# Layer 0's scan as a second row of stages, half an image ahead

## The chip, the cores and the metric

The kernel runs on one core of a Trainium2 chip. A core has five engines that work beside each other, each through its own instructions in order: PE (matmul), DVE, ACT and POOL (elementwise work), and SP, which issues the DMAs here. The metric is the time of one execution on the device in microseconds, as the median of several runs; smaller is better.

## The reference

The input is eight images of 64 x 64 tokens with 192 channels. Two layers follow each other.

Layer 0 projects to 384 channels, runs a 3 x 3 depthwise convolution with SiLU, and then a chunked state-space scan in two directions (six heads of 64 channels, 32 states, one decay per head and token). The result is gated with SiLU, projected, and an MLP of 768 hidden channels follows, with residuals.

Layer 1 splits the channels. Half of them pass a branch of three convolutions with batch norms. The other half is normalized, projected to 192 channels, convolved depthwise, and scanned selectively in four directions (row and column order, each forwards and backwards):

```python
def step(h, t):
    u_t, d_t, b_t, c_t = t
    h = jnp.exp(d_t[..., None] * A) * h + (d_t * u_t)[..., None] * b_t[:, :, None, :]
    return (h, jnp.einsum('bkdn,bkn->bkd', h, c_t))
```

Here d_t is a softplus of a projection, A is a constant for each of 192 channels and 16 states, and 4096 tokens are scanned. The four results are summed, normalized, gated, projected, and laid beside the branch's channels with a residual.

## The kernel before, in words

The backbone is `selective_scan` (L1167). It cuts the scan of one image into 8 steps of 1024 tokens (four forwards, four backwards), each step into 3 tiles of 128 channel-directions, each tile into 16 units of 8 channels x 16 states: 384 units an image, 3072 in all. For one unit q:

- `fetch` (L1314) loads delta, repeated over the states, into dA, four units ahead and into five buffers; `decay` makes exp(delta A) of it on ACT.
- `spread` (L1324) forms delta u, repeated over the states, with two matmuls from three bf16 terms (`dus`) into dB in PSUM. There are two dB buffers.
- `weigh` (L1342) multiplies dB by the B rows on DVE; `scan` (L1347) runs the recurrence on DVE into h and multiplies h by the C rows on POOL.
- `gather` (L1365) sums over the states with matmuls, for four units at once and two units behind; `store` writes y to DRAM.

`prepare` (L1249) makes delta and delta u of the next tile during the current one: softplus on ACT and POOL for all 1024 tokens, delta to DRAM, delta u in three bf16 terms to DRAM, and twelve copies back into `dus`. Its pieces are placed by half-units 0 to 31 of the tile; delta u's terms go out at 20, its copies at 23, and the first matmul that needs them stands at 30. `project` makes B, C and delta's rank terms of the next step.

All other work is written as Python generators that yield their PE cost in microseconds, or None for "no more in this half-unit". The order of instructions on each engine is fixed by the order in which the pieces are called (`pin`); no scheduler changes it. `Beside` (L1130) holds one list of such stages. In each half of a unit `half` gives it a credit, the image's total cost over its half-units, and runs the first stage until the credit is spent or it yields None. Beside image b's scan run, one after another: for image b+1 layer 0's convolution (`conv0`), layer 0's scan (`ssd`, 32 chunks of 128 tokens, four chunks in flight through five steps), its MLP (`mlp0`); for image b-1 the branch (`conv_branch`), with `scan_sums` on the side, and `scan_outputs`; and for image b+1 `scan_inputs` and `transposed`, which write the scan's input u to DRAM. Before the next image's first load, `finish` issues at once what is left. The first image's stages run alone ahead of the scan, and the last image's sums and outputs alone behind it.

PSUM has eight banks. dB takes four. The other four are handed out in turn by `Shared.one` (L87); eight of them are in turn while the first image's stages run alone.

Of the kernel before, what the change touches and what calls it, by code (L numbers as in the profile page):

```python
# [16 lines left out]
HH = WW = 64  # L17
# [12 lines left out]
S = 64  # L30
Q = 2 * S
NC = L // Q
GC = 8
# [8 lines left out]
NXP = 4 * NS + 2 * RK  # L42

# [31 lines left out]
class Shared:  # L75
# [5 lines left out]
    def __init__(self, tc):  # L81
        self.tc, self.nc, self.pin = tc, tc.nc, tc.keep_in_program_order
        self.k = {}
        self.singles = []
        self.side = None

    def one(self, name):  # L87

        self.singles.append(self.singles.pop(0))
        return self.singles[-1].tile([128, 512], F32, tag="n", name=name)  # L90

    def aside(self):

        for piece in self.side or ():
            if piece is None:
                return True
        self.side = None
        return False
# [10 lines left out]
def setup(cx, cp, dp, p0, p1):  # L109
# [122 lines left out]
    for n, c0, c1 in (("xa", 0, 128), ("xb", 128, DI), ("za", DI, DI + 128), ("zb", DI + 128, 2 * DI)):  # L232
# [3 lines left out]
        nc.vector.tensor_copy(k["bias_" + n][: c1 - c0], ps[: c1 - c0, 0:1])  # L236
    nc.vector.tensor_scalar_mul(k["in_proj"], k["in_proj"], ln_g)
# [37 lines left out]
    k["xrows"] = dp.tile([L, INNER0], F32, tag="xrows", name="xrows")  # L275
    k["prows"] = dp.tile([L, 2, NP0], F32, tag="prows", name="prows")
    k["yrows"] = [dp.tile([L, INNER0], F32, tag=f"yrows{d}", name=f"yrows{d}") for d in range(2)]
# [49 lines left out]
def conv0(cx, x):  # L327

    nc, pin, k = cx.nc, cx.pin, cx.k
    NP, R2 = NB // 2, 2 * RB  # L330
    with cx.pool("cw0") as wp, cx.pool("v0", 2) as vp:
# [13 lines left out]
        first = vp.tile([CH, 2, R2 * WW], F32, tag="xt", name="first")[:, :, :WW]  # L345
# [3 lines left out]
        def load(p):  # L349

            n = min(R2, HH - 1 - p * R2)
            xts[p] = vp.tile([CH, 2, R2 * WW], F32, tag="xt", name="xt")
            at = (p * R2 + 1) * WW
            pin(nc.sync.dma_start(
                out=xts[p][:, :, : n * WW], in_=x[:, at : at + n * WW].rearrange("(a p) l -> p a l", p=CH)
            ))

        def rows_in(j, src, n, at):
# [8 lines left out]
            ))  # L367

        def project(p, j):
# [5 lines left out]
            for b in range(2):  # L375
                n = min(RB, HH - 1 - p * R2 - b * RB)
                if n < RB:
                    pin(nc.gpsimd.memset(pad[:, R2 + 1, :], 0.0))
                rows_in(j, xts[p][:, :, b * RB * WW : (b * RB + n) * WW], n, 2 + b * RB)
                yield 2.4  # L380

        def convolve(p, j):
            pss = [cx.one("ps_cv") for i in range(2)]
            yield from depthwise(cx, pss, [diag[0:64, j], diag[64:128, j]], pads[j])
            for i, ps in enumerate(pss):
                xc = xcs[p, 2 * j + i] = vp.tile([128, 512], F32, tag="xc", name="xc", bufs=7)
                pin(nc.scalar.activation(xc, ps, AF.Silu, bias=k["cb"][:, 2 * j + i : 2 * j + i + 1]))
            cx.exp_again()

        def turn(p, q):  # L390

            here = slice(q * 128, (q + 1) * 128)
            xo = vp.tile([128, 2, INNER0], F32, tag="xo", name="xo")
            po = vp.tile([128, 2, 2 * NP0], F32, tag="po", name="po")
            for g in range(2):
                ps = cx.one("ps_x")
                for i in range(3):
                    pin(nc.tensor.transpose(ps[:, i * 128 : (i + 1) * 128], xcs[p, 3 * g + i][:, here], k["ident"]))
                pin(nc.scalar.copy(  # L399
                    xo[:, :, g * 192 : (g + 1) * 192].rearrange("t b (i c) -> t b i c", i=3),  # L400
                    ps[:, : 3 * 128].rearrange("t (i b c) -> t b i c", b=2, c=64),
                ))
                yield 0.6
            pss = [cx.one("ps_p") for b in range(2)]
            for i in range(2 * NJ):
# [6 lines left out]
                if i % 3 == 2:  # L412
                    yield 1.4
            for b in range(2):
                pin(nc.scalar.copy(po[:, b, :], pss[b][:, : 2 * NP0]))
            yield None
            for rows, t in ((k["xrows"], xo), (k["prows"].rearrange("l k m -> l (k m)"), po)):
                at = p * R2 * WW
                dst = rows[at : at + R2 * WW].rearrange("(b q t) c -> q t b c", b=2, t=128)[q]
                pin(nc.sync.dma_start(out=dst, in_=t))  # L420
# [18 lines left out]
def ssd(cx):  # L439
# [7 lines left out]
    nc, pin, k = cx.nc, cx.pin, cx.k  # L447
    K2 = 2 * NH
    chunks = [slice(i * S, (i + 1) * S) for i in range(2)]
    states_of = [slice(d * N0, (d + 1) * N0) for d in range(2)]  # L450

# [3 lines left out]
    with cx.pool("g0", 2) as gp, cx.pool("s0", 2) as sp:  # L455
        H = sp.tile([2 * N0, NH, HP], F32, tag="H", name="H", bufs=4)
        pin(nc.sync.dma_start(out=H, in_=k["p0_h0"].rearrange("n (h p) -> n h p", p=HP)))
        state = {0: H}
        groups, st = {}, {}

        def group(g):

            both = gp.tile([128, GC, 2, 2, N0], F32, tag="both", name="both")
            raw = gp.tile([128, GC, 2, NH], F32, tag="raw", name="raw")
            for d in range(2):
                for i, (at, dims) in enumerate(token_rows(k["prows"], d, g * GC, GC)):
                    def rows(col, n):
                        return bass.AP(k["prows"].tensor, k["prows"].offset + at + d * NP0 + col, dims + [[1, n]])

                    for bc in range(2):  # L470
                        pin(nc.sync.dma_start(out=both[chunks[i], :, bc, d, :], in_=rows(bc * N0, N0)))
# [1135 lines left out]
```

## Time and profile before

| What | us |
| --- | --- |
| Median of 3 runs (17,945.96 to 18,016.35) | 17,987.26 |
| Profiled execution, its own time | 17,986.38 |
| Span of its instructions | 17,984.4 |
| First scan of the selective scan starts | 981 |
| Last one ends | 17,754 |
| Busy PE, DVE, POOL, ACT | 14,375.7, 12,309.3, 12,008.5, 10,711.9 |
| One scan on DVE (L1352), 3072 of them | 2.343 |
| One product h C on POOL (L1356), 3072 of them | 2.354 |
| One product dB B on DVE (L1345), 3072 of them | 1.218 |

A line of the profile's groups gives the source line, the engine, the operation, what it writes and reads, shapes, count, busy time and mean duration, and then the time its engine stood idle ahead of it with what ended that. A line of a window answer gives the stretch, its length, each engine's busy time with the number of instructions in brackets, the share of PE's clock that was granted, the mean busy share of the 16 DMA engines, and GB/s. A line of the waits reads: who waited, for whom, microseconds in total, how often, the longest. "SPq" is SP's queue. Busy shares are averages over stages with different limits, so the stages have to be looked at one by one.

### The profile page before, as it was taken

To read this page: it belongs to the slowest core of one execution; us is meant where nothing else is said; L and a number is where in the kernel's file an instruction comes from. 1 tells how busy PE (TensorE), PEld (TensorE's weight loads), DVE (VectorE), ACT (ScalarE), POOL (GpSimd) and SP (SyncE) were. 2 spreads that over 40 slices of the span, in tenths; PEclk is the share of its full clock that TensorE was granted. 3 is DMA by queue.
4 is the path that set the end of the run, shared out by engine and by line. 5 is a ranking of instruction groups with operands and counts; after the bars stand their busy time and mean duration, and the time that the engine had idled before them with its cause. 6 is when DMAs were issued, how large, how long until landed. Compare 5 with 4: busy or idle time off the path is not lost. (4 is left out here: it accounts for less than half of the span.)

```text
span 17984.4 us, 224777 instructions
## 1 busy us (share of the span) xinstructions
PE 14375.7 (80%) x76904; PEld 5676.6 (32%) x76904; DVE 12309.3 (68%) x9392; ACT 10711.9 (60%) x18482; POOL 12008.5 (67%) x6437
## 2 busy tenths in 40 slices
PE   8977788788877888778878788787888778868776
PEld 4623332343223431334313342233422334211111
DVE  2167787776667766677657775677766777667785
ACT  2464676466664756647566485664756557555654
POOL 3168776776668755687657875678755786657774
PEclk9987788789787887878878798787987779877676
DMA  3277777777677776777767777777776777677785
GB/s 85 75 201 177 189 190 202 168 193 199 170 195 174 192 194 164 196 176 201 186 170 188 176 199 185 184 188 178 197 183 178 184 183 198 180 194 190 184 196 143
DMA packets 1600969, 3238.93 MB, mean 180 GB/s; under 512 B 391580, under 2 KB 869396, under 8 KB 1596244
## 3 DMA queue, kind: packets, MB, share of 16 engines
q1 hardware_dynamic: 1599828, 3224.55, 71.2%
q8 instruction: 614, 10.06, 0.3%
q14 instruction: 527, 4.32, 0.1%
HBM read 2545.63 MB, written 678.18 MB: 179 GB/s over the span
## 5 line engine op out<-in xcount | busy, mean ns | idle before, releaser
L1356 POOL TENSOR_TENSOR h<-h,bc 128x1023 f32<-128x1023 f32 x3072 | 7223.5, 2354 | 3926.6 <-DVE h L1352 3412.2
L1352 DVE TENSOR_TENSOR_SCAN h<-dA,carry,dB 128x1024 f32<-128x1024 f32 x3072 | 7198.8, 2343 | 624.0 <-ACT dA L1322 188.7
L1345 DVE TENSOR_TENSOR dB<-dB,bc 128x1024 f32<-128x1024 f32 x3072 | 3741.5, 1218 | 2996.7 <-PE dB L1330 2948.1
L1322 ACT ACTIVATE dA<-dA,neg_a 128x1024 f32<-128x1024 f32 x3072 | 3486.8, 1135 | 797.5 <-DMA dA<-dld 795.3
L1374 PE MATMUL acc<-h,gather 128*32 128x512 f32 x12288 | 2479.9, 758 | 525.7 <-POOL h L1356 203.2
L1378 ACT COPY y<-acc 128x512 f32<-128x512 f32 x1536 | 886.5, 577 | 1908.7 <-PE acc L1374 1891.4
L1330 PE MATMUL dB<-dus,spread 24*128 24x512 bf16 x6144 | 1418.8, 430 | 365.3 <-DVE h L1352 283.8
L795 PE MATMUL ps_c<-p,conv_w 96*96 96x512 f32 x2304 | 1250.9, 670 | 120.5 <-ACT p L816 105.8
L1330 PEld LDWEIGHTS <-spread 24*128 24x128 bf16 x6144 | 317.6, 93 | 2607.9 <-issue 1700.3
L620 PE MATMUL ps_y<-dtx,M 64*64 64x64 f32 x12288 | 824.3, 267 | 393.5 <-DVE Hn L611 387.1
L1363 ACT ACTIVATE h<-h,bc 128x1 f32<-128x1 f32 x3072 | 905.1, 295 | 163.3 <-ACT carry L1362 3.8
L620 PEld LDWEIGHTS ps_y<-dtx,M 64*64 64x64 f32 x12288 | 691.6, 177 | 572.8 <-issue 349.5
L1374 PEld LDWEIGHTS acc<-h,gather 128*32 128x32 f32 x12288 | 321.2, 119 | 1690.8 <-issue 836.4
L319 PE MATMUL ps_cv<-pad,diag 64*64 64x512 f32 x6912 | 849.9, 611 | 5.6 <-ACT xo L399 2.8
L1276 POOL TENSOR_TENSOR w<-w,e 128x1024 f32<-128x1024 f32 x192 | 452.6, 2357 | 510.7 <-ACT carry L1362 423.7
L757 PE MATMUL ps_m<-h,w 128*96 128x256 f32 x3072 | 750.1, 392 | 30.2 <-DVE gT L715 20.4
L739 PE MATMUL ps_h<-o,w 96*128 96x256 f32 x3072 | 749.3, 397 | 4.3 <-ACT zs L697 1.7
L1362 ACT COPY carry<-h 128x1 f32<-128x1 f32 x3072 | 575.4, 187 | 250.9 <-DVE h L1352 248.1
L739 PEld LDWEIGHTS ps_h<-o,w 96*128 96x128 f32 x3072 | 585.6, 196 | 174.6 <-issue 62.3
L795 PEld LDWEIGHTS ps_c<-p,conv_w 96*96 96x96 f32 x2304 | 367.5, 177 | 814.8 <-issue 703.3
L555 PE MATMUL ps_d<-R,after 128*128 128x384 f32 x1024 | 554.8, 631 | 84.6 <-DVE M L575 36.8
L106 ACT ACT_TABLE_LOAD x481 | 617.1, 1283 | 8.2
(244 smaller groups left out, 22124.1 us busy)
## 6 DMA issues: line engine op xcount, KB each, us to landing
dA<-dld SPq DMA_DIRECT2D x3072, 512.0 KB
dud<-terms SPq DMA_DIRECT2D x192, 768.0 KB
dus<-dud SPq DMA_DIRECT2D x2304, 64.0 KB
bc<-bcd SPq DMA_DIRECT2D x256, 512.0 KB
X<-xrows SPq DMA_DIRECT2D x1024, 96.0 KB
yrows<-yo SPq DMA_DIRECT2D x1024, 96.0 KB
y<-yrows SPq DMA_DIRECT2D x256, 384.0 KB
u<-u SPq DMA_DIRECT2D x192, 512.0 KB
```

The costliest lines, as they stand in the source:

```text
L319: pin(nc.tensor.matmul(ps[64 * b : 64 * (b + 1)].rearrange("p (h w) -> p h w", w=WW), lhsT=diag[:, t, :], rhs=pad[64 * i : 64 * (i + 1), b ...
L620: pin(nc.tensor.matmul(psy[d][here, h * HP : (h + 1) * HP], lhsT=M[here, d, h, :], rhs=dtx[here, d, h, :], start=True, stop=d == 1,))
L739: pin(nc.tensor.matmul(ps[:, n * T : (n + 1) * T], lhsT=w1[:, a, (f + n) * 128 : (f + n + 1) * 128], rhs=o[:, a, :], start=a == 0, stop=a ...
L795: pin(nc.tensor.matmul(ps.rearrange("p (h w) -> p h w", w=WW), lhsT=w[:, t, :], rhs=pad[:, dy : dy + RB, dx : dx + WW], start=t == 0, stop ...
L1322: pin(nc.scalar.activation(dAs[q], dAs[q], AF.Exp, scale=k["neg_a"][:, steps[m][1], t, i : i + 1]))
L1330: pin(nc.tensor.matmul(dBs[q][:, half, :], lhsT=k["spread"][at : at + 3 * UD, :], rhs=du_of[n][at : at + 3 * UD, i // 2, :], start=True, s ...
L1345: pin(nc.vector.tensor_mul(dBs[q], dBs[q], of(q)[0]))
L1352: pin(nc.vector.tensor_tensor_scan(order(h, g), order(dA, g), order(dB, g), carry, ALU.mult, ALU.add))
L1356: pin(nc.gpsimd.tensor_mul(h[:, rest], h[:, rest], C_[:, rest]))
L1363: pin(nc.scalar.activation(end, end, AF.Identity, scale=C_[:, last : last + 1]))
L1374: pin(nc.tensor.matmul(ps[32 * v : 32 * (v + 1)], lhsT=k["gather"], rhs=hs[q - 3 + v][:, here], start=True, stop=True))
L1378: pin(nc.scalar.copy(y[:, here], ps))
```

## The change

`ssd` is rewritten and gets a row of its own in `Beside`. It works one chunk at a time in `front` and `back`, with a None after nearly every matmul group; in the prologue a chunk's back and the next one's front take turns (`together`). Its groups hold four chunks (`GC`) where they held eight, its pools stay open for the whole kernel, and layer 0's rows in DRAM exist twice. Each half-unit, `half` first gives the ssd row a share and then the other row the rest of the credit. A stage can name what it comes after. The other row runs `conv0` two images ahead, then the sums and outputs of the image before, then `mlp0`, `scan_inputs` and `transposed` of the next image; the branches are spread over images 0, 5, 6 and 7 as one, one, two and four. Image 1's `conv0` is woven into image 0's `ssd` in the prologue. `one` and `drop` hand PSUM banks out in the order in which their last readers were issued. `prepare` works in two halves of 512 tokens; delta u's second half goes out at half-unit 24, the copies for the tile's first eight units at 25, and those for the other eight in the next tile (`lay_du`). y is copied and stored in halves. Several tiles in the other stages have fewer buffers.

```diff
     def one(self, name):
-        self.singles.append(self.singles.pop(0))
-        return self.singles[-1].tile([128, 512], F32, tag="n", name=name)
...
+        home = self.free.pop(0)
+        t = home.tile([128, 512], F32, tag="n", name=name)
+        self.home[id(t)] = t, home
+        return t
+
+    def drop(self, *tiles):
+        for t in tiles:
+            self.free.append(self.home.pop(id(t))[1])
...
+    def front(c):
...
+        yield 0.4
+        yield None
+        bc = sp.tile([2 * N0, 2, Q], F32, tag="bc", name="bc", bufs=bufs)
+        pin(nc.scalar.copy(bc.rearrange("p i t -> p (i t)"), ps[: 2 * N0, : 2 * Q]))
+        cx.drop(ps)
...
+            yield 1.1
+            yield None
+            pin(nc.scalar.activation(flat(M[:, d]), some, AF.Exp))
+            cx.drop(ps)
...
+    def back(c):
+        next(coming, None)
...
+            yield 0.5
+            yield None
+            pin(nc.vector.tensor_add(H, ps[: 2 * N0, :INNER0].rearrange("p (h c) -> p h c", c=HP), H))
+            cx.drop(ps)
...
+    if not two:
+        for c in range(NC):
+            yield from front(c)
+            yield from back(c)
+        return
+    yield from front(0)
+    for c in range(NC):
+        yield from together(back(c), *([front(c + 1)] if c + 1 < NC else []))
...
     def half(self):
-        self.cx.aside()
         self.credit = min(self.credit, self.rate) + self.rate
-        while self.credit > 0.0 and self.stages:
-            for cost in self.stages[0]:
-                if cost is None:
-                    return
-                self.credit -= cost
-                if self.credit <= 0.0:
-                    return
-            self.stages.pop(0)
+        if self.ssds:
+            key, _, _, mine = self.ssds[0]
+            theirs = 0.0
+            for other in self.others:
+                if other[2] == key:
+                    break
+                theirs += max(other[3], 0.0)
+            mine = max(mine, 5.0)
+            self.share = min(self.share + (self.rate - 0.65) * mine / (mine + theirs), 2.0)
+            if self.share > 0.0:
+                spent = self.run(self.ssds, self.share)
+                self.share -= spent
+                self.credit -= spent
+        if self.credit > 0.0:
+            self.credit -= self.run(self.others, self.credit)
...
-            dl, e, w, b = (wp.tile([128, LC], F32, tag=v, name=v) for v in ("dl", "e", "w", "b"))
...
+            for at, here in zip((0, 12), halves):
+                dl, e, w, b = (wp.tile([128, 512], F32, tag=v, name=v) for v in ("dl", "e", "w", "b"))
...
+                yield at + 12
+                pin(nc.sync.dma_start(out=dud.rearrange("s p l -> p s l")[:, :, here], in_=terms))
+            yield 25
+            lay_du(n, 0)
+
+        def lay_du(n, part):
+            dus = np_.tile([128, UN // 4, 512], BF16, tag=f"dus{part}", name=f"dus{part}", bufs=1)
             for half in range(2):
                 for odd in range(2):
                     at = 32 * (2 * odd + half)
                     for v in range(3):
+                        rows = dud_of[n][v][64 * part : 64 * (part + 1), halves[half]]
                         pin(nc.sync.dma_start(
...
+                if at == 1:
+                    lay_du(n, 1)
...
                 for half in range(2):
+                    beside.half()
                     next(gathering, None)
-                    beside.half()
...
+    branches = list(range(B))
+    for b in range(B):
+        if b + 2 < B:
+            add("conv0", b + 2)
+        if b > 0:
+            add("sums", b - 1, ("scan", b - 1))
+            add("outputs", b - 1)
+        for _ in range({0: 1, B - 3: 1, B - 2: 2, B - 1: 4}.get(b, 0)):
+            add("branch", branches.pop(0))
+        if b + 1 < B:
+            beside.add(("ssd", b + 1), lambda b=b: ssd(cx, b + 1, gp, sp), ("conv0", b + 1))
+            add("mlp0", b + 1, ("ssd", b + 1))
+            add("inputs", b + 1)
+            add("transposed", b + 1)
+
+    def new_image(b, units):
+        rates, halves = [], 0
+        for i in range(b, B):
+            halves += 2 * (units if i == b else U_IMAGE)
+            key = ("transposed", i + 1) if i + 1 < B else ("branch", B - 1)
+            rates.append(beside.left(key, OWN * halves) / halves)
+        beside.rate = max(rates)
```

## The prediction

> **What bounds the kernel now.** The page first: no engine is full, and the chain that ended last names none.
>
> ```profile
> PE 14375.7 (80%) x76904; PEld 5676.6 (32%) x76904; DVE 12309.3 (68%) x9392; ACT 10711.9 (60%) x18482; POOL 12008.5 (67%) x6437
> PE 14%; DMA 10%; ACT 7%; POOL 6%; DVE 6%; issue 3%; SPq 1%; DVEq 0%; POOLq 0%; ACTq 0%
> ```
>
> So I cut the third image (5118 to 7315 us) by stage with the stage windows. In order: layer 0's convolution (48 scan units), the start of its scan (16), its scan (80), hand-over (17), its MLP (81), branch and sums (65), outputs and layer 1's inputs (80). The eighth row is a late stretch with hardly anything beside the selective scan (49 units). The units are the same windows' counts of L1352.
>
> ```profile
> core 0: us, PE busy (x) PEld busy (x) DVE busy (x) ACT busy (x) POOL busy (x), PEclk, DMA share, GB/s
> 5118.00:5333.00 215.00, 193.77 (x1282) 73.01 (x1282) 168.61 (x96) 157.29 (x284) 153.61 (x75) 0.89 0.79 203
> 5333.00:5454.00 121.00, 75.21 (x594) 36.51 (x594) 68.36 (x59) 57.56 (x126) 79.42 (x55) 0.70 0.68 156
> 5454.00:5943.00 489.00, 361.77 (x3452) 167.59 (x3452) 382.94 (x385) 222.32 (x434) 421.18 (x262) 0.78 0.71 176
> 5943.00:6045.00 102.00, 76.03 (x384) 45.83 (x381) 65.28 (x52) 68.55 (x103) 62.18 (x30) 0.82 0.77 197
> 6045.00:6423.00 378.00, 337.97 (x1472) 185.37 (x1471) 308.58 (x223) 310.18 (x498) 273.51 (x122) 0.92 0.77 197
> 6423.00:6822.00 399.00, 325.24 (x929) 98.89 (x927) 229.13 (x136) 190.63 (x341) 227.13 (x118) 0.88 0.72 191
> 6822.00:7315.00 493.00, 390.33 (x1479) 98.47 (x1478) 312.68 (x214) 329.72 (x524) 283.61 (x145) 0.76 0.67 170
> 17400.00:17600.00 200.00, 121.79 (x346) 22.96 (x346) 169.06 (x98) 112.63 (x205) 157.54 (x70) 0.69 0.81 193
> ```
>
> A unit costs 4.48 us beside the convolution and 4.67 beside the MLP, with PE 89 to 90% busy; 6.11 beside layer 0's scan, with POOL at 86% and PE only at 74%; 7.56 where that scan starts; 6.1 to 6.2 in the last two stages; 4.08 alone, where DVE is the bound at 85%. Each stage has its own limit. Whole images, and then the waits:
>
> ```profile
> 5118.00:7315.00 2197.00, 1760.33 (x9582) 705.66 (x9582) 1535.57 (x1160) 1336.26 (x2306) 1500.64 (x802) 0.83 0.72 183
> 16024.00:17754.00 1730.00, 1279.08 (x3327) 273.60 (x3326) 1363.53 (x807) 989.20 (x1766) 1261.68 (x589) 0.69 0.78 190
> DVE dB L1345 <- PE dB L1330: 2948.1, 959, 111.3
> DVE Hm L595 <- POOL Hm L579: 365.4, 115, 9.2
> PE ps_y L620 <- DVE Hn L611: 387.1, 166, 5.7
> PE dB L1330 <- DMA dus<-dud: 70.7, 19, 30.2
> SPq L1317 <- DVE h L1352: 4266.5, 1528, 18.2
> ```
>
> DVE loses most to PE's dB: PE stands in other stages' work when the scan needs it. A middle image holds 1760 us of PE in 2197, the last only 1279 in 1730.
>
> **What the skill says.** The Trainium skill, Perfetto Trace Analysis, Optimization Strategy: where the most contended engine changes between regimes, interleaving the regimes may help; the rows above are such regimes. TensorE: Matmul & The Clock Gate, Part 1 (The HAM clock gate): idleness lowers PE's clock. The trace agrees: 0.69 alone, 0.78 beside layer 0's scan, 0.92 beside the MLP. I take no gain from it. Perfetto Trace Analysis, Identifying the Most-Contended Engine, warns that PE's busy share is a poor measure of its peak; I use it only as a ratio, before to after. The price of a table switch is used below.
>
> **The change, part by part.**
>
> (1) *Two rows.* Computation stays; layer 0's scan moves. In the built order of the changed kernel the scans of images 1 to 7 occupy units 8-216, 227-534, 546-906, 918-1281, 1293-1653, 1666-2084 and 2097-2517 of 3072: nearly always one in progress, a chunk per 11 units where it was 3.5. Convolutions run an image further ahead, MLPs behind their scans. The conv branches leave the middle images: one in image 0, one in 5, two in 6, four in 7. I counted each image's instructions at the mean of their row before: PE 1849, 1681, 1679, 1667, 1665, 1615, 1580 and 1510 us (the same count before: 1538, six of 1735 to 1797, 1188; the third image measured 1760). A middle image keeps DVE near 1536, POOL near 1540, ACT near 1385.
>
> Price: what share can PE hold? Unmixed stages gave 74% to 90%. At 85% a middle image takes 1661/0.85 = 1954 us, with DVE and POOL at 79%, ACT at 71% and DMA at 82% (now 0.73 x 2187 = 1597 us of DMA an image). DVE and ACT are then below their 82% of the MLP stage and POOL below its 86%, but none at once with the others; I take 85%, not 89%, for that. Sum: image 0 1849/0.85 = 2175; five middle images 9772; image 6 1580/0.85 = 1859; image 7, bound by DVE, 384 x 4.45 = 1709 (now 4.51, and PE rises to 88%). Together 15,515.
>
> Image 0 has one lump: unfinished inputs are issued at once at its end, with 172 us of PE in 16 units. Its work is inside 2175. The other images finish their inputs in time, so the gap of some 50 us at each image's end goes; it is inside the 85% too.
>
> (2) *Prologue.* Image 1's convolution comes before the scan, woven into image 0's layer 0 scan. Alone it took 202 us with PE busy 179; that scan stage took 272 us with PE busy 236, so there are only 36 us to hide in: +143 to +202, I take +165. The selective scan starts at 981 + 165 = 1146. The tail stays 17,984 - 17,754 = 231 us (rounded).
>
> (3) *Halves.* Six ACT operations a tile become twelve: a 1024-element cast takes 1.04 us and a 512-element copy 0.577, so +0.11 x 6 x 192 = 127 us. Six POOL operations: 2.13 to 2.36 us against an estimated 1.15 to 1.264 twice, +0.17 x 6 x 192 = 200 us. Table loads go from 1197 to 1364: 167 x 1.283 = 214 us, or 444 with the drain that ScalarE: Activation LUTs, What ACT_TABLE_LOAD costs, adds (2.66 us a switch; the trace shows only the 1.283). Groups of four chunks add 32 sets of some nine ACT operations at 0.27 and six on POOL at 0.39: under 160 us in all. ACT ends near 11,300 of 17,200 us, 66%: hidden by slack, and priced at the above if ACT becomes the bound.
>
> (4) *SP.* 20,550 DMA issues for 14,246: y stores doubled (+3072), dus (+2304), the rest small. At 0.29 to 0.54 us each SP's own time rises from 6.4 to about 8.5 ms. SP now waits 4266 us for dA buffers alone, so this hides there, on average. Bytes stay.
>
> (5) *Hand-over at each tile.* This is where halving adds a wait. Before, the last du term goes out in half-unit 20 and its spread copies in 23, for the spread matmul in 30. Afterwards they go out in 24 and 25. In the timelines of SP and PE du's issue stood 22.9 us (median) before that matmul, 14.5 in the fastest twentieth. Four half-units less, at 2.55 us, leave 12.7; the parts of the chain need about 13 (4.6 until du has landed, 6 for twelve copies, 2.4 until the last has). So half the tiles fall short, by 0 to 5 us. Behind the spread matmul stands all of PE, then DVE's dB. Bounds: 0 (each copy is half as large now, the other twelve come a unit later) to 6 us a tile. I take 1.3 x 191 = 248 us.
>
> (6) *Banks.* Reuse by last reader: matmuls that follow at once on the reader of their bank rise from 776 to 1301 of some 7,200 in the built order, since a slow row holds a bank over many half-units. Against it, PE and DVE lose the waits within layer 0's scan above (365 + 387 us), as its updates now stand further apart. From +500 (525 at about 1 us) to -750; I take zero.
>
> Sum: 1146 + 15,515 + 231 + 248 = 17,140, and 60 for stages that open on a weight load: **17,200 us**. It stands against the profiled execution, 17,986 us round a span of 17,984, and the median of the runs is 17,987, so no correction is due.
>
> **Rivals.**
>
> *The mix runs to the DMA's limit.* The largest DMA share in a 200 us window was 0.84; 1597/0.84 = 1900 us an image. With images 0, 6 and 7 at 2054, 1800 and 1680 this gives 15,034 + 1146 + 231, about 16,450. For it: PE at 90% in two stages. Against: 6300 more issues on the one queue that feeds the scan.
>
> *The waits only change place.* PE holds its present 80.5%: (1849 + 8305 + 1580)/0.805 = 14,576, + 1709 + 1377 + 80 = about 17,740. For it: banks, more semaphore waits, POOL and ACT hops half as far apart (ACT waits for POOL's du 573 us already). It would equal the kernel before at 78.7%.
>
> *The tile hand-over decides* (the other side): PE stands at each tile's first spread until du's copies land. It turns slower beyond (17,987 - 16,892)/191 = 5.7 us a tile; at its 6 us and over, 18,100. For it: 12.7 us left where 13 are needed, behind a busier queue. Against: this wait was 70.7 us in all before, and the shortfall worked out is far from 5.7.
>
> That the change does not do what it says is excluded by the order of instructions.
>
> **How the numbers follow.** Forecast 0.52 (its own range 16,900 to 17,550), DMA limit 0.17, waits change place 0.20, hand-over 0.11. Leaving out half of the first rival's lower tail and most of the last case: 16,650 to 17,850. Half a per cent (90 us) is about what can be told from no change: faster is below 17,897. That holds for the first two cases, most of the third and none of the last: 0.85; within, 0.07; slower, 0.08.
>
> **What would show it.** Right: windows over a middle image of 1900 to 2020 us with PE near 85% and POOL, DVE near 79%, without stretches at 6 us a unit; first scan near 1146; image 7 near 1700. Step 5 wrong: PE dB waiting for dus far above 250 us. Step 6 wrong: PE or its weight loads waiting for ACT's copies. Step 4 wrong: ACT dA waiting for its DMA far above the present 795 us. The prediction fails most likely by PE's share.

## The result, and the profile after

The changed kernel takes 19,145.29 us (median of 4 runs, 19,123.47 to 19,179.44) against 17,973.05 us for the kernel before on the same chip: a ratio of 1.0652, with a 95% interval of 1.0623 to 1.0680. It is 6.5% slower. The forecast was 17,200 us, its range ended at 17,850, and "slower" had a chance of 0.08: the prediction was wrong in its sign.

The page's busy line and the chain that ended last, of the kernel after (span 19,157.8 us):

```profile
PE 15141.6 (79%) x77288; PEld 5886.3 (31%) x77288; DVE 12285.5 (64%) x9392; ACT 11147.3 (58%) x20089; POOL 12215.1 (64%) x7781
DMA 2%; PE 2%; DVE 1%; ACT 1%; POOL 1%; issue 0%; SPq 0%; DVEq 0%; ACTq 0%; POOLq 0%
```

DVE does the same work as before. PE is busy 766 us longer, though there are only 384 more matmuls. The windows of the kernel after show image 0, the third image (image 2) and image 7:

```profile
core 0: us, PE busy (x) PEld busy (x) DVE busy (x) ACT busy (x) POOL busy (x), PEclk, DMA share, GB/s
1230.00:3624.00 2394.00, 1920.38 (x11410) 811.82 (x11411) 1563.74 (x1244) 1371.06 (x2543) 1601.18 (x1062) 0.81 0.64 165
5931.00:8194.00 2263.00, 1771.81 (x9665) 708.50 (x9666) 1534.33 (x1170) 1397.03 (x2503) 1519.36 (x956) 0.79 0.68 177
17060.00:18919.00 1859.00, 1443.61 (x3932) 364.30 (x3926) 1367.84 (x807) 1059.95 (x1983) 1308.42 (x767) 0.77 0.71 183
```

The third image was to take 1954 us, with 1661 us of PE work at a share of 85%. It takes 2263 us, with PE busy for 1772 us, a share of 78%. POOL and DVE are at 67% and 68%. The clock fell from 0.83 to 0.79. Images 0 to 5 and 7 are each longer than before, by 42 to 443 us; image 6 is as long. Where the engines wait gives the first hint (waits of the kernel after, some of the larger ones of POOL, ACT, PE and DVE):

```profile
POOL w L1387 <- ACT carry L1476: 1036.8, 225, 21.5
POOL dt L507 <- DMA raw<-prows: 702.1, 55, 38.1
POOL w L1387 <- ACT w L1385: 334.8, 77, 83.4
ACT terms L1398 <- POOL du L1392: 618.1, 186, 17.7
ACT e L1377 <- PE ps_dt L1373: 558.9, 251, 25.2
PE ps_u L533 <- POOL da L523: 353.4, 59, 29.1
PE dB L1443 <- DMA dus<-dud: 140.4, 64, 29.4
DVE dB L1459 <- PE dB L1443: 4054.4, 1190, 106.7
```

The same waits of the kernel before (those of dB and dus stand in the prediction):

```profile
POOL w L1276 <- ACT carry L1362: 423.7, 162, 11.8
POOL dt L479 <- DMA raw<-prows: 162.3, 9, 64.0
ACT terms L1291 <- POOL du L1283: 351.8, 90, 9.7
ACT e L1267 <- PE ps_dt L1262: 122.2, 61, 11.9
POOL w L1276 <- ACT w L1274: 86.9, 1, 86.9
PE ps_u L503 <- POOL da L495: 175.1, 8, 23.5
```

POOL now stands at the head of its queue for a step of `prepare` (w) or for a load that layer 0's scan has asked for a moment ago (dt), 55 times for 12.8 us on average instead of 9 times. The lines that name carry mean the hand-over inside `prepare` too: in the trace a w that waited starts 77 ns (median) after ACT's w of L1385, which it reads, and carry is what ACT ends at that moment. Everything queued behind on POOL, the product h C for one, is held up with it, and what needs that product (gather on PE) can be late in turn. Summed over all that POOL does apart from h's product (idle gaps over 0.3 us), its idle time inside the scan went from 1,122 to 2,982 us. h's own wait fell from 3,917 to 2,707. In all POOL stands 650 us longer.

A *hop* is from here on the distance, in half-units, between the step in which one engine is asked to make a result and the step in which another is asked to use it. Two theories came out of the waits. **H**: the new schedule has hops that are too short, one half-unit or none (both in the same piece), so that the user stands. **M**: the mixing itself is at fault, the scan of layer 0 beside every other stage, which takes the full clock away from the dense ones. The expectations below call PE TensorE and DVE VectorE.

### The profile page after: what moved, and what is told of

The parts are those of the page before. It is cut to its first block, busy times and chain, and to the rows that moved or that the text cites. A ratio compares the mean times of both kernels' runs of the same rounds, so it can differ in the third digit from the quotient of the medians.

```text
span 19157.8 us, 237594 instructions
## 1 busy us (share of the span) xinstructions
PE 15141.6 (79%) x77288; PEld 5886.3 (31%) x77288; DVE 12285.5 (64%) x9392; ACT 11147.3 (58%) x20089; POOL 12215.1 (64%) x7781
## 5 line engine op out<-in xcount | busy, mean ns | idle before, releaser
L1466 DVE TENSOR_TENSOR_SCAN h<-dA,carry,dB 128x1024 f32<-128x1024 f32 x3072 | 7194.9, 2342 | 506.0 <-ACT dA L1435 252.1
L1459 DVE TENSOR_TENSOR dB<-dB,bc 128x1024 f32<-128x1024 f32 x3072 | 3751.0, 1221 | 4332.0 <-PE dB L1443 4054.4
L1435 ACT ACTIVATE dA<-dA,neg_a 128x1024 f32<-128x1024 f32 x3072 | 3486.3, 1135 | 634.0 <-DMA dA<-dld 631.4
L1488 PE MATMUL acc<-h,gather 128*32 128x512 f32 x12288 | 2183.5, 714 | 574.8 <-POOL h L1470 197.1
L848 PE MATMUL ps_c<-p,conv_w 96*96 96x512 f32 x2304 | 1376.3, 727 | 140.4 <-ACT p L869 113.3
L1387 POOL TENSOR_TENSOR w<-w,e 128x512 f32<-128x512 f32 x384 | 487.4, 1269 | 1371.8 <-ACT carry L1476 1036.8
L322 PE MATMUL ps_cv<-pad,diag 64*64 64x512 f32 x6912 | 986.2, 665 | 41.0 <-ACT xc L393 24.3
L791 PE MATMUL ps_h<-o,w 96*128 96x256 f32 x3072 | 845.3, 430 | 93.2 <-ACT M L600 32.9
L660 PE MATMUL ps_y<-dtx,M 64*64 64x64 f32 x12288 | 706.8, 239 | 60.2 <-ACT y L1492 26.7
L742 PE MATMUL ps_z<-xt,w_z 96*128 96x256 f32 x1536 | 499.6, 485 | 287.6 <-DMA xt<-in_x_dram 107.8
L660 PEld LDWEIGHTS ps_y<-dtx,M 64*64 64x64 f32 x12288 | 583.0, 151 | 311.5 <-issue 128.4
L1400 POOL TENSOR_TENSOR du<-du,terms 128x512 f32<-128x512 f32 x384 | 443.2, 1154 | 358.5 <-ACT terms L1398 278.6
L628 PE MATMUL ps_s<-xw,both 64*32 64x384 f32 x2048 | 545.8, 617 | 138.9 <-POOL xw L586 41.8
```

The lines of the kernel that those rows point to most:

```text
L322: pin(nc.tensor.matmul(ps[64 * b : 64 * (b + 1)].rearrange("p (h w) -> p h w", w=WW), lhsT=diag[:, t, :], rhs=pad[64 * i : 64 * (i + 1), b ...
L660: pin(nc.tensor.matmul(ps[here, h * HP : (h + 1) * HP], lhsT=M[here, d, h, :], rhs=dtx[here, d, h, :], start=True, stop=d == 1,))
L791: pin(nc.tensor.matmul(ps[:, n * T : (n + 1) * T], lhsT=w1[:, a, (f + n) * 128 : (f + n + 1) * 128], rhs=o[:, a, :], start=a == 0, stop=a ...
L848: pin(nc.tensor.matmul(ps.rearrange("p (h w) -> p h w", w=WW), lhsT=w[:, t, :], rhs=pad[:, dy : dy + RB, dx : dx + WW], start=t == 0, stop ...
L1435: pin(nc.scalar.activation(dAs[q], dAs[q], AF.Exp, scale=k["neg_a"][:, steps[m][1], t, i : i + 1]))
L1459: pin(nc.vector.tensor_mul(dBs[q], dBs[q], of(q)[0]))
```

## The experiments

| Run | Median, us | Ratio to before, 95% interval |
| --- | --- | --- |
| after | 19,145 | 1.0652, 1.0623 to 1.0680 |
| after, groups paced | 18,814 | 1.0442, 1.0425 to 1.0459 |
| after, hops in prepare spaced | 18,898 | 1.0483, 1.0460 to 1.0507 |
| after, both ("mended") | 18,538 | 1.0290, 1.0272 to 1.0309 |
| before + halves | 18,360 | 1.0194, 1.0171 to 1.0217 |
| before + halves, hops spaced | 18,055 | 1.0046, 1.0032 to 1.0059 |
| before + groups of four | 18,471 | 1.0272, 1.0255 to 1.0289 |
| before, POOL's steps one half-unit later | 18,044 | 1.0035, 1.0021 to 1.0049 |
| before, spread early | 17,919 | 0.9964, 0.9946 to 0.9983 |
| before + halves spaced, gather three behind | 18,247 | 1.0145, 1.0128 to 1.0162 |
| mended, layer 0's scan unshared | 18,534 | 1.0307, 1.0289 to 1.0324 |
| mended, spread early | 18,474 | 1.0277, 1.0258 to 1.0296 |
| mended, banks last in, first out | 23,750 | 1.3219, 1.3189 to 1.3249 |
| before + PE work | 18,124 | 1.0097, 1.0064 to 1.0129 |
| mended + PE work | 18,805 | 1.0467, 1.0439 to 1.0496 |
| mended + POOL work | 18,647 | 1.0381, 1.0358 to 1.0405 |
| mended + ACT work | 18,757 | 1.0439, 1.0415 to 1.0463 |
| mended + DVE work | 19,029 | 1.0586, 1.0560 to 1.0611 |

The kernel before took 17,962 to 18,006 us beside these runs, so points of the ratio are compared, not microseconds. "Halves" are the two halves of 512 tokens in `prepare`.

**Mending the hops in the changed kernel.** First the groups: `front` takes two steps of the coming group in a row. Here it takes one, and the group starts a chunk earlier.

```diff
-        if c % GC == 1 and c // GC + 1 < NC // GC:
+        if c % GC == (1 if two else 0) and c // GC + 1 < NC // GC:
             coming = group(c // GC + 1)
-        for i in range(2):
+        for i in range(1 + two):
             next(coming, None)
```

> The changed kernel (19,145 us), with the steps of a group of chunks (its loads, POOL's dt add, ACT, POOL's da, PE's ps_u, POOL's toend) each put one half chunk after the other, where it has two steps back to back. Theory H (hops too short: POOL and PE stand at the head of their queues for data that was asked for a moment before, and everything behind them is late): POOL's dt wait of 702 us and PE's ps_u wait on da of about 350 us go, and the time falls by 150 to 450 us, to 18,700 to 19,000. Rival M (the mixing itself: the scan of layer 0 beside every other stage leaves TensorE at half clock more often, 43% of the scan against 38%): those waits go too, but the time stays within 100 us of 19,145, since the same waits fall elsewhere, and the granted clock stays at 0.79.

Then the slots of `prepare`, which count half-units from the start of each half tile:

```diff
                 cx.drop(ps)
-                yield at + 2
+                yield at + 1
                 pin(nc.scalar.activation(e, e, AF.Exp, scale=-1.0))
                 pin(nc.scalar.activation(w, e, AF.Identity, bias=k["one"]))
-                yield at + 3
                 pin(nc.scalar.activation(b, w, AF.Ln))
                 pin(nc.scalar.activation(w, w, AF.Identity, bias=k["minus"]))
-                yield at + 4
+                yield at + 3
                 pin(nc.gpsimd.tensor_sub(w, w, e))
                 pin(nc.gpsimd.tensor_sub(b, b, w))
-                yield at + 5
                 pin(nc.gpsimd.tensor_add(dl, dl, b))
...
-                yield at + 6
+                yield at + 5
                 pin(nc.sync.dma_start(out=dld[:, here], in_=dl))
...
-                yield at + 7
                 pin(nc.scalar.copy(terms[:, 0, :], du))
-                yield at + 8
+                yield at + 7
                 pin(nc.gpsimd.tensor_sub(du, du, terms[:, 0, :]))
                 yield at + 9
                 pin(nc.scalar.copy(terms[:, 1, :], du))
-                yield at + 10
+                yield at + 11
                 pin(nc.gpsimd.tensor_sub(terms[:, 2, :], du, terms[:, 1, :]))
```

> The changed kernel, with the hops between ACT and POOL in prepare two half units long where they are one (the ACT steps together in the slot after the copies out of PSUM, then POOL's four, then ACT, POOL, ACT, POOL in every second slot; both halves end where they ended). Theory H: POOL's wait for w (1,282 us) and ACT's for terms (1,017 us) fall by half, and the time falls by 200 to 600 us, to 18,550 to 18,950. Rival M: those waits shrink, the time stays within 100 us of 19,145 and the clock at 0.79.

> Both edits together. Theory H: 400 to 900 us below the changed kernel, 18,250 to 18,750, and POOL's time at the head of its queue back from 2,982 us to under 1,700 (it was 1,122 before the change). Rival M: within 150 us of 19,145 although POOL's waits fall as far.

The paced groups give 2.1 points back, the spaced hops 1.7, both 3.6: more than half of the 6.5, and they nearly add. In the mended kernel the waits of the kernel after read:

```profile
POOL w L1386 <- ACT w L1384: 281.8, 76, 83.0
POOL dt L507 <- DMA raw<-prows: 118.4, 12, 14.9
POOL w L1386 <- ACT carry L1473: 73.7, 24, 12.5
PE ps_u L533 <- POOL da L523: 55.8, 11, 15.3
ACT terms L1395 <- POOL du L1390: 451.5, 192, 9.5
ACT e L1377 <- PE ps_dt L1373: 530.7, 224, 25.7
```

POOL's wait on dt fell from 702 to 118 us and that of w under carry's name from 1,037 to 74; its idle time apart from h's product fell from 2,982 to 987 us. What `prepare` still does in one piece, a matmul and its copy out of PSUM (ACT e behind ps_dt), makes ACT wait almost as long as in the kernel after. Removing short hops thus gave back 3.6 points, as H has it, and M's "the time stays" is out. The clock came back a little too, 0.791 to 0.800.

**The halves and the groups alone, on the kernel before.** `prepare`, `lay_du`, spread's operand, y and its stores are taken from the changed kernel, and nothing else:

```diff
-            dl, e, w, b = (wp.tile([128, LC], F32, tag=v, name=v) for v in ("dl", "e", "w", "b"))
+            for at, here in zip((0, 12), halves):
+                dl, e, w, b = (wp.tile([128, 512], F32, tag=v, name=v) for v in ("dl", "e", "w", "b"))
...
+                if at == 1:
+                    lay_du(n, 1)
```

> The kernel before (17,973 us) with nothing of the change but the halves: prepare, lay_du, the spread's operand, y and its stores as in the changed kernel. The prediction's step (3): hidden, so 17,900 to 18,100. Theory H: a third to a half of the loss is in it, 18,300 to 18,700. Rival M: 17,900 to 18,150, as in the prediction, since the halves alone mix nothing.

The same with the slots of the second diff above:

> The kernel before with the halves alone, and the hops between ACT and POOL two half units long as in the run with spaced hops of the changed kernel. Theory H: the halves' loss (360 us) is their hops, and most of it goes: 18,050 to 18,200; no faster than before. What the rows and the groups of four add is then read against the run with both edits (18,538): 340 to 490 us, of which the longer prologue (first scan at 1,219 against 981) is 240. Rival: the halves cost by their number (twice the instructions and table loads), not by their hops: it stays at 18,300 to 18,400.

Groups of four chunks in the kernel before:

```diff
-GC = 8
+GC = 4
...
-            if coming is not None:
+            for i in range(2 if coming is not None else 0):
                 next(coming, None)
```

> The kernel before with groups of four chunks as in the changed kernel, two steps of a group back to back in each chunk, and nothing else of the change. Pacing the same steps in the changed kernel gave 332 us back. Theory H (it is the back to back steps): 100 to 350 us slower than before, 18,060 to 18,310, with POOL's wait for raw in front of dt (94 us before) over 300. If they hurt only where the scan of layer 0 runs beside everything: within 80 us of before.

Alone, the halves cost 1.9% and the groups 2.7%, where the prediction had called both hidden. With spaced hops the halves cost 0.5%: three quarters of their price was in the hops, and the doubled number of instructions is the rest at most. Table loads are no rival here: the halves have 1206 of them, with spaced hops 1221, and the kernel before 1197. The groups' price is larger than expected, and needs no second row. Of its some 480 us, 55 lie ahead of the first scan. Waits of the kernel before with groups of four:

```profile
POOL dt L479 <- DMA raw<-prows: 643.5, 62, 63.0
DVE Hn L611 <- POOL Hn L597: 717.8, 155, 14.1
PE ps_y L620 <- DVE Hn L611: 811.0, 180, 14.4
```

POOL waits for raw 62 times where it waited 9 times. Hn's product stands a few places behind dt on POOL, DVE waits for it 718 us where it waited 178 (43 waits of over 1 us, 428 us together, fall within 12 us behind a wait at dt; none did before), and PE stands at ps_y for 811 us where it stood 387. A chain from the DMA over POOL and DVE to PE starts at one load whose first use stands directly behind its issue.

**The same cure on the kernel before.** All of POOL's steps in `prepare`, and what follows them, one half-unit later:

```diff
-            yield 5
+            yield 6
             pin(nc.gpsimd.tensor_sub(w, w, e))
...
-            yield 23
+            yield 24
...
             dus = np_.tile([128, UN // 2, 512], BF16, tag="dus", name="dus")
```

> The kernel before with its whole tiles, the first subtraction of POOL in prepare and all after it one half unit later (the hop from ACT's logarithm to POOL two half units where it is one). Theory H: its POOL wait for w (422 us) falls by more than half, and the time by 30 to 200 us, to 17,800 to 17,970. Rival (the wait costs nothing at the rate of the kernel before, as POOL has slack there): within 30 us of before.

This missed: 0.35% slower. Two waits of that run say why:

```profile
POOL w L1276 <- ACT carry L1362: 420.6, 162, 11.8
PE dB L1330 <- DMA dus<-dud: 280.1, 99, 30.1
```

w's wait hardly changed (423.7 before), and the dus copies, one half-unit later, hold PE for 280 us instead of 71. Counted in half-units the hop was doubled. But on POOL little was put into it: in the traces one product h C stands between ACT's step and w in the kernel before, and still one in this run, since slots 5 and 6 lie between the same two products. In the kernel after there is none (for 382 of 384 w), with spaced hops one. What stands between maker and user on the user's own queue thus describes these runs better than the count of slots. The cure above also drew ACT's steps together, and which of the two helps most was not taken apart.

**Is it the mix?** In the mended kernel the ssd row takes all of the credit that it can use, instead of a share:

```diff
-            self.share = min(self.share + (self.rate - 0.65) * mine / (mine + theirs), 2.0)
+            self.share = min(self.share + self.rate - 0.65, 2.0)
```

> The changed kernel with both edits (18,538), and layer 0's scan takes all of the credit that it can use at each half unit instead of a share over all of the image: its chunks end at about half of an image, and the MLP and the next stages then run without it. Same work, same hops, same banks. If the long mix is what makes TensorE's work dearer (it is at half clock for 41.5% of the scan, 38.0% before the change), the denser stages get their clock back: 18,250 to 18,450. If it neither helps nor hurts: 18,480 to 18,600. If the mix does help, as the prediction's step (1) has it: over 18,650.

1.0307 against 1.0290: no difference that the intervals show. Layer 0's scan of images 2 to 7 then takes some 202 units in place of 308 to 422, and nothing is gained or lost in all. The length of the mix is worth nothing either way. The mix does go with a lower clock: over images 1 to 5 this run was granted 0.77 in the units beside layer 0's scan and 0.81 in the others, the kernel before 0.77 and 0.84.

**Banks.** In the mended kernel a bank goes back to the head of the free list:

```diff
-            self.free.append(self.home.pop(id(t))[1])
+            self.free.insert(0, self.home.pop(id(t))[1])
```

> The changed kernel with both edits (18,538), and a bank that has been read is handed out first instead of last, so that nearly every user takes the bank whose last copy was issued just before it. If the order in which banks are handed out matters (the change deals them by last reader; the prediction put this at zero, between +500 and -750), this doubles the suspected cost: over 18,800, and TensorE's waits for ACT's copies grow. If not, 18,480 to 18,620.

The order in which banks are handed out is no small matter: 29 points. Waits of this run:

```profile
PE ps_g L607 <- ACT M L600: 418.4, 163, 10.3
PE ps_d L596 <- ACT bc L590: 400.5, 174, 13.5
DVE dB L1456 <- PE dB L1440: 7469.0, 1799, 137.4
```

PE stands for the copy out of the bank that it was handed; it is also busy longer, 17,624 us against 14,955, at a clock of 0.693. Of the 5,215 us by which the span grows, 585 lie ahead of the first scan. The Trainium skill, Perfetto Trace Analysis, Optimizing Tensor Performance (Matmuls), asks that independent matmul groups rotate through banks; this run shows what it costs when they don't. It doesn't price the change's own order, which is the opposite one. Handing out in a fixed turn, as the kernel before does, was not tried under the second row, since that row holds a bank over half-units.

**Which engine's work sets the pace?** In the kernel before, the first matmul of each spread is issued twice:

```diff
-                pin(nc.tensor.matmul(
-                    dBs[q][:, half, :], lhsT=k["spread"][at : at + 3 * UD, :], rhs=du_of[n][at : at + 3 * UD, i // 2, :],
-                    start=True, stop=True,
-                ))
+                for again in range(2 - half):
+                    pin(nc.tensor.matmul(
+                        dBs[q][:, half, :], lhsT=k["spread"][at : at + 3 * UD, :], rhs=du_of[n][at : at + 3 * UD, i // 2, :],
+                        start=True, stop=True,
+                    ))
```

> The kernel before with one more matmul per unit (the first matmul of spread is issued twice, the second writing over the first): 3,072 x 385 to 432 ns = 1,180 to 1,330 us of TensorE work at the place in its queue on which VectorE's dB waits. If TensorE's queue sets the pace at a share of 80%, every microsecond of work costs 1 to 1.25: 19,150 to 19,650. If its idle 3,321 us can take work (the prediction's premise, share up to 85%): 18,300 to 19,000. If another chain sets the pace: under 18,300.

It cost 1.0%, 174 us of 18,000. The dB matmuls' busy time went from 1,418.8 to 2,174.4 us: 0.23 us for one, where a PE that sets the pace at a share of 80% would cost 1.25. (PE's whole busy time rose by 579 us only, since other matmuls got shorter at a clock of 0.822 after 0.815; by that count the price is 0.3.) The same on the mended kernel, and one more instruction per unit on each of the other engines behind h's product (128 x 128 on POOL, 128 x 256 on ACT and DVE):

```diff
             pin(nc.gpsimd.tensor_mul(h[:, rest], h[:, rest], C_[:, rest]))
+            pin(nc.gpsimd.tensor_add(more, more, more))
```

On ACT the added line is `nc.scalar.copy(more, more)`, on DVE `nc.vector.tensor_add(more, more, more)`.

> The changed kernel with both edits (18,538), the first matmul of spread issued twice: what one microsecond of TensorE work costs there. On the kernel before it cost 146 us for 1,180 us of instructions (754 us of TensorE's own busy time). If TensorE's work doesn't set the pace here either: 18,600 to 18,800. If the rows have made it the bound, as step (1) prices it (work divided by share): 19,300 and more.

> The changed kernel with both edits, and one more addition of 128 x 128 per unit on POOL behind h's multiplication (about 0.4 us each, 1,200 us in all). If the pace is set by the hand-overs to and from POOL and ACT, POOL's work costs over half of its length: 19,100 to 19,800. If POOL has slack (67% busy): under 18,800.

> The changed kernel with both edits, and one more copy of 128 x 256 per unit on ACT (0.3 to 0.4 us each, about 1,100 us in all). If the pace is set by the hand-overs to and from POOL and ACT: 19,000 to 19,700. If ACT has slack (61% busy): under 18,800.

> The changed kernel with both edits, and one more addition of 128 x 256 per unit on VectorE behind the scan (0.3 to 0.4 us each, about 1,100 us). VectorE waits 3,644 us for dB and so should have slack: under 18,850. If its own chain of weigh and scan sets the pace: 19,300 and more.

What was added, by group: the dB matmuls before and with the double issue, and the added instruction on POOL, ACT and DVE, each from its own run:

```profile
L1440 PE MATMUL dB<-dus,spread 24*128 24x512 bf16 x6144 | 1502.4, 432 | 378.6 <-DVE h L1463 212.2 <-DMA dus<-dud 159.2 <-DMA y<-y 2.0
```

```profile
L1441 PE MATMUL dB<-dus,spread 24*128 24x512 bf16 x9216 | 2255.4, 427 | 299.6 <-DVE h L1464 184.7 <-DMA dus<-dud 111.6 <-DVE dB L1457 1.3
```

```profile
L1470 POOL TENSOR_TENSOR more<-more 128x128 f32<-128x128 f32 x3072 | 1224.2, 399 | 0.0
```

```profile
L1470 ACT COPY more<-more 128x256 f32<-128x256 f32 x3072 | 1192.4, 388 | 0.0
```

```profile
L1470 DVE TENSOR_TENSOR more<-more 128x256 f32<-128x256 f32 x3072 | 2081.8, 678 | 0.0
```

Against the mended kernel's 1.0290 the points are 1.8, 0.9, 1.5 and 3.0, or some 320, 165, 270 and 530 us of 18,000. For one us of added busy time (753, 1224, 1192, 2082 us) that is 0.4 on PE, 0.1 on POOL, 0.2 on ACT and 0.25 on DVE. By the rise of each engine's whole busy time, in which overlaps count once (602, 1,083, 892 and 1,829 us), it is 0.5, 0.15, 0.3 and 0.3. PE came in 5 us above the range for "doesn't set the pace" and far below the other, POOL and ACT inside "has slack", and DVE between its two cases. Every engine has a price and none has the price of a bound. DVE's addition moved the time most, 3.0 points, though DVE is only 66% busy; but a part of what it added is stretch (see the last section).

**Where dB stands in PE's queue.** spread(q + 1) is issued at the head of the unit, ahead of the half-unit's other work; once in the kernel before, once in the mended one:

```diff
                 for half in range(2):
+                    if half == 0 and q + 1 < U:
+                        spread(q + 1)
...
                             carry_on(q - 1)
-                        if q + 1 < U:
-                            spread(q + 1)
                         scan(q)
```

> The kernel before with spread(q + 1) at the head of a unit, ahead of the half unit's other work. VectorE waits 2,948 us for this dB while TensorE is in other stages' work. If TensorE's place in its queue is what VectorE lacks: dB's wait halves and the time falls by 200 to 600 us, 17,400 to 17,800. If TensorE then only waits longer for VectorE's scan to give the dB buffer back: 17,900 to 18,300.

> The same move of spread in the changed kernel with both edits (18,538): 18,000 to 18,350 if the place in TensorE's queue is what VectorE lacks, 18,450 to 18,850 if not.

On the kernel before, the wait of DVE is a third smaller, and a good part of it is now PE's:

```profile
DVE dB L1345 <- PE dB L1330: 1990.2, 649, 110.5
PE dB L1330 <- DVE h L1352: 843.7, 480, 11.0
```

PE's wait on DVE for the dB buffer was 283.8. What is left is 0.36% (0.17 to 0.54): the one version here that is faster than both kernels, by less than what was held to be measurable. In the mended kernel the intervals overlap.

**Gather one unit later.** The halves free memory; the kernel before with spaced halves has `AHEAD, BEHIND = 4, 3` instead of `4, 2`, with one h buffer more.

> The kernel before with the halves and their spaced hops (18,055), whose freed memory goes to one more h buffer: gather runs three units behind the scan instead of two. If TensorE's wait at gather (512 us before, for ACT's and POOL's h) is on the path: 17,500 to 17,900, faster than both kernels. If not, within 80 us of 18,055.

This missed in sign: PE's idle time ahead of gather fell from 565.9 to 301.4 us, and the kernel is one point slower than without the move. PE waits more for the dB buffer (355 against 242 us), and the granted clock is 0.801 against 0.822. Here too a wait that was taken away was paid elsewhere; which step pays first was not found.

## Why the prediction was wrong

**(3) Halves and groups: the step that failed.** It counted instructions (127 us on ACT, 200 on POOL, 214 of table loads, under 160 for groups) and called them "hidden by slack". POOL's busy time rose by 207 us and the table loads to 1364, as counted (though the halves alone add only 9 of the 167), and slack does hide most of such work (1,224 us on POOL cost some 165). But the step priced no waits. The halves give POOL and ACT their steps at a shorter distance; the groups use a load directly behind its issue. Alone on the kernel before these cost 1.9% and 2.7%; in the changed kernel, where the two are mended by distance alone, 3.6 of the 6.5 points come back. The prediction had seen a part of it: "POOL and ACT hops half as far apart" stands in the rival of waits that change place, as a reason for a share of 80.5%, and was left without a price. That rival is nearest in kind, but with 17,740 us it was 1,400 short.

**(1) The price of an image failed too.** The PE work was counted as 13,246 us and, image 7 apart, priced at a share of 85%. Two terms were off. The share is 13,929/17,689 = 78.7%; and PE's work itself took 13,929 us, 5% more than counted at the mean durations of before, at a lower clock. Together they turn the predicted 15,515 us into 17,689. More than its figure, the form was wrong: work divided by a share takes PE for the engine that sets the pace. One us of added PE work costs 0.2 to 0.5. By the same token, moving the branches out of the middle images, some 100 us of PE each by that count, could save little. This is seen in the windows of images 1 to 6 together and of the fourth image (image 3), first of the mended kernel, then of the kernel before with spaced halves:

```profile
3523.00:16469.00 12946.00, 10397.03 (x53595) 4035.86 (x53596) 9114.94 (x6839) 8266.20 (x14744) 9032.13 (x5627) 0.79 0.70 184
7903.00:10065.00 2162.00, 1740.65 (x9531) 689.79 (x9529) 1531.00 (x1167) 1410.34 (x2515) 1524.75 (x960) 0.79 0.70 185
```

```profile
2970.00:16078.00 13108.00, 10457.27 (x57283) 4238.92 (x57286) 9222.04 (x6960) 8205.31 (x14713) 9155.79 (x5670) 0.83 0.70 185
7353.00:9534.00 2181.00, 1737.56 (x9596) 702.80 (x9598) 1536.74 (x1160) 1370.20 (x2458) 1526.21 (x947) 0.84 0.71 185
```

The six images have 6% fewer matmuls, but PE is busy almost as long, at a lower clock, and 162 us are saved, 27 an image (from 15 us longer in the third to 84 shorter in image 6). A second row was to fill PE's waits. But PE's order is fixed: a piece of the other row that is queued behind a wait stands as well. The rows would then fill only the gaps that the order leaves, not those in which the head of the queue stands. No run shows this last step by itself.

**(2) The prologue was too small by 84 us.** The first scan starts at 1230 instead of the predicted 1146 (981 before); the window up to it has PE busy for 1046 us. The prediction hid 36 of the 202 us that image 1's convolution had taken alone; nothing was hidden, and 47 us came on top. Groups of four alone put the first scan of the kernel before at 1,036, 55 us later, which is about as much.

**(4) SP: right.** 20,550 issues did not hurt: ACT's wait for dA's loads is 631.4 us, where it was 795.3.

**(5) The hand-over: right in kind, too large.** PE's wait for dus rose from 70.7 to 140.4 us, so by 70 and not by 248; and the rival that it decides is out. Its slack was as thin as worked out, though: one half-unit later in the kernel before costs 209 us of waiting.

**(6) Banks: not settled.** The bounds of +500 and -750 were stated for the order by last reader. Its reverse costs 29 points, so banks are a strong lever, but no run has the fixed turn beside the second row.

**The sums and the other rival.** The DMA rival's own terms add up to 16,411 us, not 16,450; it is out, as no image of the kernel after has a DMA share over 0.71. The rival of waits says that it would equal the kernel before at a share of 78.7%; with the 80 us that its sum holds it is 79.2%. The 60 us for weight loads stand without a working.

The mended kernel and the kernel before with spaced halves differ in the rows, the banks, where branches stand, and groups of four. By their spans that is 18,544.2 against 18,034.0, 510 us: the first scan 248 later, image 0 306 longer and image 7 104 longer (both got work from elsewhere), the six images between 162 shorter, the tail 16 longer. Work was moved out of the middle, where it costs little, to the prologue and the two ends. This says where the rest of the loss lies; which of the four differences makes it was not taken apart. Why PE's clock is lower in the middle, 0.79 against 0.83, stays open: beside layer 0's scan it is low in the kernel before as well, but a scan of half the length left the middle at 0.79.

## What to carry to other kernels

When a step is cut in two so that its buffers shrink, count the distance between each producer and its consumer on every queue, not only the added instructions: two steps one slot apart on two in-order engines cost more here (1.5 points) than all the instructions that came with them (0.5). Ask the price of work before pricing by it: add one small instruction per loop to each engine, and see which one moves the time. And keep a load and its first use apart when the user sits at the head of an engine that others wait for: half a chunk between them took POOL's wait from 702 to 116 us here.

## What the runs showed of the hardware

Summed from the clock records of the trace, the granted clock between the first and the last scan is only ever 0.5 or 1.0. The time at full clock is nearly the same in the changed kernel and in its three mended versions (groups, hops, both): 10,011, 9,997, 9,993 and 9,997 us. With both, this stretch is 611 us shorter, and 597 of them come off the half-clock time, which goes from 7,678 to 7,081 us. In these runs the waits that went away were waits at half clock. That isn't so everywhere: with layer 0's scan unshared the full-clock time is 9,900 us in a stretch of the same length, and with the reversed banks it is 8,048. That there are just two values is as the Trainium skill has it (TensorE: Matmul & The Clock Gate, Part 1, What's actually happening).

The addition of 128 x 256 on DVE took 399 ns in the median, but 678 in the mean and 9,329 at most, while h's product beside it on POOL went from 2,354 to 2,398 ns. The Trainium skill, GPSIMD Engine Reference, Specifications, puts POOL's SBUF interfaces down as shared with DVE, with contention for DVE instructions that have two SBUF inputs; this instruction has two. The trace fits: 698 of the 3,072 additions took over 0.5 us, and a POOL instruction ran during 99% of their time, against 51% of that of the others. The scan (2,342 ns with the addition and without) did not stretch. No run separates the cause further.
